# Three sums in DRAM for the experts' outputs of a token, where there were four

## The chip, the cores and the metric

The kernel runs on one NeuronCore of a Trainium2 chip, as one launch. The time is that of the device in microseconds (us): the kernel before took 3354.55 us, the median of 9 runs (3341.1 to 3369.14). One further execution was recorded by the profiler and took 3357.96 us; the durations below are from it.

## What is computed

Two transformer-like layers over `x` of 4 sequences x 2048 tokens x 256 features, float32:

```python
x = x + delta_rule_attention(layernorm(x))     # 16 heads of 16, a recurrence over the tokens
x = x + moe(layernorm(x))                      # this is the part that the change touches
x = x + state_space_scan(layernorm(x))         # state of 16, a recurrence over the tokens
x = x + quantized_linear(layernorm(x))         # values rounded to a 6-bit grid in blocks of 32

def moe(x):                                    # 32 experts, 8 of them for each token
    topk_idx, topk_w = gate(x)
    outs = down(silu(gate_proj(x)) * up(x))    # per expert; 256 -> 128 -> 256
    final = (gathered(outs, topk_idx) * topk_w).sum(1)
    return final + shared_mlp(x)
```

Each token's result in `moe` is therefore a sum of eight weighted expert outputs, of the shared network's output and of the residual `x`.

## The kernel before

The tokens are worked on in 16 blocks of 512 (128 tokens of each of the four sequences). The blocks fall into four groups of 3, 5, 5 and 3 blocks.

**First phase** (the span's first 2255 us or so). `delta_layer` does the attention of block after block. `Router.route` follows one block behind: it chooses the experts, writes the block's residual plus shared output into the first sum (`rt["sums"](i, 0)`, line 791) and copies a block of zeros into each of the other sums (lines 792 to 795). Then it scatters each token's row, eight times, into `rows`, a DRAM table that is sorted by expert (line 799, GpSimd, called POOL below). Further DMAs per group give every sum 128 spare rows of zeros and pad the table (lines 815 to 822). When a group of blocks is complete, the expert tiles of that group may begin. 160 tiles (64 of group 0 and 96 of group 1, `BEGUN`) are woven into the first phase.

**Experts.** A tile is two half tiles of 128 rows, each of one expert. `load` fetches 384 KB of weights, 128 KB of rows and each row's weight and token number per half (lines 925, 929, 930), `widen` computes the hidden layer (line 946 on TensorE, PE below; 951 on ScalarE, ACT; 952 on VectorE, DVE), and `narrow` the output (line 959 on PE). ACT scales it by the router's weight into the tile `ye` (line 964), and POOL starts an indirect DMA that *adds* the 128 rows of 256 floats to rows of a sum in DRAM (line 967):

```python
y = work.tile([P, 2, DM], F32, name="ye", bufs=self.ahead)
...
nc.gpsimd.indirect_dma_start(
    rt["sum"][g][(2 * t + n) % NACC][:, :],
    bass.IndirectOffsetOnAxis(ap=wrow[:, n, 1:2].bitcast(U32), axis=0),
    y[:, n, :], None, bounds_check=GROUPS[g] * TOK + P - 1, compute_op=ALU.add,
)
```

Such an indirect DMA is called a scatter below. Each group has `NACC` sums, and its scatters go to them in turn. Two scatters into one sum may touch the same token, so the framework lets a scatter wait until the one before it *into the same sum* has landed. That wait stands in POOL's queue, which is worked off in order. `ye` has `ahead` buffers: 2 tiles in the first phase, 6 tiles (12 scatters) in the second. ACT may write a buffer again when its scatter has landed.

**Second phase.** `last_layers` takes block after block through three stages, which are woven together. `stage_sum` (lines 1077 to 1085) loads sum 0 of a block as `x` (line 998) and then one `part` after the other, and adds them on DVE:

```python
for m in range(1, NACC):
    part = work.tile([P, NB, DM], F32, name="part", bufs=3)
    nc.sync.dma_start(part, rt["sums"](i, m))
    nc.vector.tensor_tensor(x, x, part, op=ALU.add)
    yield
```

`stage_scan` and `stage_ffn` do the last two lines of the reference; they give POOL three operations per block (lines 1094, 1095, 1147). The other 160 expert tiles (groups 2 and 3) are woven into blocks 0 to 12. Blocks 13 to 15 are group 3's own: `stage_sum` of block 13 reads sums to which the very last tile adds.

Within both phases the order of the instructions on each engine is set by a scheduler, which works from a timeline of its own. Plain DMAs are started by SyncE (SP); all engines' queues are in order.

Of the kernel before, what the change touches and what calls it, by code (L numbers as in the profile page):

```python
# [49 lines left out]
BEGUN = [64, 96, 0, 0]  # L50
NROW = NE * REG + P
DR = DM + 2 * NE
NACC = 4
XB = 2
AHEAD = 0.8
KC = 4
# [565 lines left out]
class Router:  # L622
# [8 lines left out]
    def __init__(self, ctx, sh, layer, rt):  # L631
# [125 lines left out]
        def stage_route(i, x, count, views):  # L757
# [33 lines left out]
            nc.sync.dma_start(rt["sums"](i, 0), x)  # L791
            for m in range(1, NACC):
                layer.beside(nc.sync.dma_start(
# [14 lines left out]
        def route(i, x):  # L808
            g = GROUP_OF[i]
            if i == GFIRST[g]:  # L810
# [7 lines left out]

                for m in range(NACC):
                    layer.beside(nc.sync.dma_start(  # L820
# [58 lines left out]
class Experts:  # L879
# [9 lines left out]
    def group(self, g, lag, lo, hi):  # L889
# [65 lines left out]
        def narrow(t):  # L955
# [7 lines left out]
            for n in range(2):  # L963
# [3 lines left out]
# [3 lines that stand above are left out]
# [13 lines left out]
def last_layers(ctx, sh, layer, xout, rt):  # L983
# [93 lines left out]
    def stage_sum(i):  # L1077
        x = load_x(i)
        x_of[i] = x
# [3 lines that stand above are left out]
# [93 lines left out]
def block_kernel(ctx: ExitStack, tc: tile.TileContext, a: dict, out: bass.AP):  # L1176
# [6 lines left out]
        "sum": [  # L1183
            [keep.tile([n * TOK + P, DM], F32, name=f"sum{g}_{m}") for m in range(NACC)]
            for g, n in enumerate(GROUPS)
# [156 lines left out]
```

## Time and profile before

| | us |
|---|---|
| median of 9 runs | 3354.55 (3341.1 to 3369.14) |
| the profiled execution | 3357.96 |
| its span, from the first to the last instruction | 3356.2 |
| busy in the span: PE / DVE / ACT / POOL | 2792.8 / 2010.2 / 1812.6 / 1735.2 |
| scatters (line 967), all on POOL | 640, 1043.4 us busy |
| last scatter started / landed | 3166.9 / 3174.2 |

"Idle before, releaser" in the profile is the idle time of an engine ahead of a group of instructions, and what ended most of it. "SPq" and "POOLq" are the queues of SP and POOL. The chain that ended last is followed back from the last instruction, at each step to what released it. A scatter's own row shows only POOL's work for it; when its data has landed is seen from the semaphore that each scatter raises 16 times, the last of which tells that it is done.

### The profile page before, as it was taken

The numbers are of one execution on the slowest core, as the hardware profiler recorded it, in microseconds if no ns is written. First come the engines' busy times: TensorE is split into PE (matmuls) and PEld (weight loads), VectorE is DVE, ScalarE is ACT, GpSimd is POOL, SyncE is SP. The second block draws the span as 40 slices with busy tenths as digits, with TensorE's granted clock in tenths as the row PEclk, the third lists the DMA queues.
The fourth block names the chain that finished last, engine by engine and source line by source line (L and its number), as shares of the span: only waits on it lengthen the run. The fifth ranks groups of instructions, "written<-read, shape, count | busy, mean of one in ns | idle before, by whom it ended". The sixth has DMA issues, their size and how long they took to land. (4 is left out here: it accounts for less than half of the span.)

```text
span 3356.2 us, 72319 instructions
## 1 busy us (share of the span) xinstructions
PE 2792.8 (83%) x24564; PEld 2095.6 (62%) x24564; DVE 2010.2 (60%) x4958; ACT 1812.6 (54%) x3640; POOL 1735.2 (52%) x1235
## 2 busy tenths in 40 slices
PE   5768886899999878999999888875898998899644
PEld 2446564676777656777677566763676777667522
DVE  4787675665656656576565645434667442764466
ACT  3544453555656555566565544543665764577432
POOL 0003224456475552746647455566667887568611
PEclk7778787999999998999999889987999999999876
DMA  2334446888898887988888889788999999999800
GB/s 86 61 64 113 109 112 182 201 217 216 202 261 219 220 217 196 233 215 226 222 196 250 203 243 233 192 251 264 305 297 293 278 302 307 302 251 295 218 24 19
DMA packets 788810, 695.92 MB, mean 207 GB/s; under 512 B 482312, under 2 KB 672024, under 8 KB 785304
## 3 DMA queue, kind: packets, MB, share of 16 engines
q1 hardware_dynamic: 669432, 522.25, 54.6%
q0 software_dynamic: 116736, 167.85, 24.0%
q8 instruction: 195, 3.19, 0.4%
q14 instruction: 175, 1.43, 0.1%
q10 hardware_dynamic: 2272, 1.19, 0.1%
HBM read 472.41 MB, written 267.53 MB: 220 GB/s over the span
## 5 line engine op out<-in xcount | busy, mean ns | idle before, releaser
L967 POOL DMA_INDIRECT sum<-ye,wrow x640 | 1043.4, 1630 | 707.9 <-ACT ye L964 498.6
L799 POOL DMA_INDIRECT rows<-xn,rows x512 | 544.3, 1063 | 420.8 <-issue 180.2
L946 PE MATMUL gu<-xe,we 128*128 128x128 f32 x5120 | 672.6, 285 | 43.2 <-ACT xe L936 35.9
L946 PEld LDWEIGHTS gu<-xe,we 128*128 128x128 f32 x5120 | 629.3, 198 | 98.6 <-ACT xe L936 47.0
L959 PE MATMUL py<-we,he 128*128 128x256 f32 x1280 | 360.5, 406 | 78.6 <-DVE he L952 78.1
L964 ACT ACTIVATE ye<-py,wrow 128x256 f32<-128x256 f32 x640 | 268.3, 472 | 242.0 <-PE py L959 165.9
L952 DVE TENSOR_TENSOR he<-he,gu 128x256 f32<-128x256 f32 x320 | 133.0, 416 | 422.1 <-ACT he L951 421.4
L934 PE MATMUL px<-ident,xg 128*128 128x128 f32 x1280 | 227.7, 289 | 120.5 <-DMA xg<-rows 116.1
L959 PEld LDWEIGHTS py<-we,he 128*128 128x128 f32 x1280 | 229.9, 197 | 138.3 <-DVE he L952 94.1
L934 PEld LDWEIGHTS px<-ident,xg 128*128 128x128 f32 x1280 | 163.8, 147 | 200.2 <-DMA xg<-rows 83.4
L936 ACT COPY xe<-px 128x512 f32<-128x512 f32 x320 | 188.2, 588 | 176.1 <-PE px L934 174.9
L951 ACT ACTIVATE he<-gu 128x256 f32<-128x256 f32 x320 | 123.5, 386 | 259.6 <-PE gu L946 257.0
L348 DVE TENSOR_TENSOR kqd<-kq,hmask 128x512 f32<-128x512 f32 x256 | 168.0, 687 | 91.3 <-PE pg L358 84.7
L263 DVE SCALAR_TENSOR_TENSOR cy<-pre,convw,cy 128x512 f32<-128x512 f32 x288 | 214.4, 749 | 3.5
L247 PE MATMUL proj<-xt,wqkv 128*128 128x512 f32 x384 | 203.7, 658 | 3.3 <-DVE rq L310 3.0
L505 PE MATMUL c<-vkm,tm 64*64 64x64 f32 x4096 | 178.2, 235 | 11.8 <-ACT vkm L490 9.5
L549 DVE TENSOR_TENSOR state<-sps,same 128x512 f32<-128x512 f32 x254 | 164.3, 681 | 32.3 <-PE sps L542 31.8
L505 PEld LDWEIGHTS c<-vkm,tm 64*64 64x64 f32 x4096 | 152.0, 146 | 49.1 <-issue 25.3
L358 PE MATMUL pg<-kqd,kq 64*32 64x128 f32 x4096 | 139.9, 301 | 42.7 <-ACT gk L365 29.3
L542 PE MATMUL sps<-ro,kr 64*128 64x128 f32 x2032 | 165.1, 308 | 7.1 <-ACT ro L535 7.1
L542 PEld LDWEIGHTS sps<-ro,kr 64*128 64x128 f32 x2032 | 138.8, 208 | 40.5 <-issue 15.8
L143 DVE BATCH_NORM_STATS2 st<-x 128x6 f32<-128x256 f32 x256 | 92.1, 414 | 104.0 <-DMA x<-in_x 102.7
(206 smaller groups left out, 4941.3 us busy)
## 6 DMA issues: line engine op xcount, KB each, us to landing
we<-in_wexp SPq DMA_DIRECT2D x640, 384.0 KB
xg<-rows SPq DMA_DIRECT2D x640, 128.0 KB
sum<-in_blank SPq DMA_DIRECT2D x48, 512.0 KB
part<-sum SPq DMA_DIRECT2D x48, 512.0 KB
rows<-in_zeros SPq DMA_DIRECT2D x132, 160.0 KB
x<-in_x SPq DMA_DIRECT2D x32, 512.0 KB
gscr<-gk SPq DMA_DIRECT2D x64, 256.0 KB
lq<-gscr SPq DMA_DIRECT2D x64, 256.0 KB
```

What stands on the lines that cost most here:

```text
L247: nc.tensor.matmul(ps, wqkv[:, k, w, c * P : (c + 1) * P], xt[:, k, :], start=(k == 0), stop=(k == NC2 - 1),)
L263: nc.vector.scalar_tensor_tensor(y, pre[:, :, k : k + T], convw[:, w, c, k : k + 1], y, op0=ALU.mult, op1=ALU.add,)
L348: nc.vector.tensor_tensor(kqd, kq[:, u0 + du, c].rearrange("p b t w -> p b (t w)") .unsqueeze(2).broadcast_to([P, NB, HH, 2 * C]), hmask.u ...
L505: nc.tensor.matmul(c0[rows, :, p * 32 : (p + 1) * 32], tmk[rows, p].rearrange("p b t -> p (b t)"), vkm[rows, :, p].rearrange("p w r d -> p ...
L542: nc.tensor.matmul(sps[h][:, h2, c, :], kr[rows, h2, c * P : (c + 1) * P], ro[rows, c * P : (c + 1) * P], start=(i == 0 and k == 0 and h2 ...
L799: layer.beside(nc.gpsimd.indirect_dma_start(views[((i - GFIRST[GROUP_OF[i]]) * NB + b) * TOPK + k], bass.IndirectOffsetOnAxis(ap=rows[:, b ...
L934: nc.tensor.transpose(px[:, c, n, :], xg[:, n, c * P : (c + 1) * P], ident)
L936: nc.scalar.copy(xt, px)
L946: nc.tensor.matmul(gu[:, v, n, :], w[n][:, o : o + P], xt[:, c, n, :], start=(c == 0), stop=(c == NC2 - 1),)
L959: nc.tensor.matmul(py[:, n, :], h[:, n, :], w[n][:, 4 * P :], start=True, stop=True)
L964: nc.scalar.activation(y[:, n, :], py[:, n, :], AF.Copy, scale=wrow[:, n, 0:1])
L967: nc.gpsimd.indirect_dma_start(rt["sum"][g][(2 * t + n) % NACC][:, :], bass.IndirectOffsetOnAxis(ap=wrow[:, n, 1:2].bitcast(U32), axis=0), ...
```

## The change

`NACC` is 3. A group has three sums; scatters go to them in turn. Per block one copy of zeros, one load of a part and one DVE addition fall away (16 of each), and per group one small copy of zeros (4). A scatter waits for the third one before it, where it waited for the fourth.

```diff
--- before.py
+++ after.py
@@ -50,7 +50,7 @@
 BEGUN = [64, 96, 0, 0]
 NROW = NE * REG + P
 DR = DM + 2 * NE
-NACC = 4
+NACC = 3
 XB = 2
 AHEAD = 0.8
 KC = 4
```

## The prediction

> **What bounds the kernel now.** I read the page first, then busy time by stage, then the chain, then POOL's waits and timeline. By stage, the second phase is the full one:
>
> ```profile
> 2255.00:3175.00 920.00, 794.91 (x4732) 616.57 (x4731) 501.81 (x1072) 554.61 (x981) 652.63 (x398) 0.94 1.03 284
> 3175.00:3356.00 181.00, 80.86 (x204) 39.76 (x204) 122.81 (x247) 47.94 (x63) 24.39 (x10) 0.69 0.11 39
> ```
>
> (columns: stretch, length, then busy us and count of PE, weight loads, DVE, ACT, POOL; granted clock, DMA share, GB/s). PE is busy 86% of it and the DMA queues together over 100%: loads are always waiting there. After 3175 only the last three blocks are left, a chain of DVE and PE work that the scatters do not touch. So whatever delays the last scatter delays the end by as much. The chain that ended last says the same:
>
> ```profile
> 3089.61 34.93 DMA sum<-ye,wrow x6
> ...
> 3125.04 19.24 DMA sum<-ye,wrow x3
> ...
> 3159.38 3.57 DMA sum<-ye,wrow
> ...
> 3166.90 7.33 DMA sum<-ye,wrow
> 3174.24 4.71 DMA part<-sum
> ```
>
> (start, us, what.) From 3090 to 3174 the end hangs on scatters alone; before that it is mostly expert matmuls with a few waits for loads. Now POOL, which starts the scatters:
>
> ```profile
> L967 POOL DMA_INDIRECT sum<-ye,wrow x640 | 1043.4, 1630 | 707.9 <-ACT ye L964 498.6
> ```
>
> ```profile
> 3101.04 1.55 POOL L967 DMA_INDIRECT sum<-ye,wrow  x1 [0.30 <-DMA sum<-ye,wrow]
> 3102.89 1.55 POOL L967 DMA_INDIRECT sum<-ye,wrow  x1 [0.31 <-DMA sum<-ye,wrow]
> 3105.32 1.55 POOL L967 DMA_INDIRECT sum<-ye,wrow  x1 [0.88 <-DMA sum<-ye,wrow]
> ...
> 3141.80 1.55 POOL L967 DMA_INDIRECT sum<-ye,wrow  x1 [1.34 <-DMA sum<-ye,wrow]
> ```
>
> A scatter costs POOL 1.55 us and some 0.30 between two: back to back, one in 1.86 us. A wait for an earlier scatter shows as the longer gaps (0.88, 1.34). They are small, because four sums are just enough, as the next part shows.
>
> **The price of a scatter's turn.** From the semaphores I took each scatter's time from its start on POOL to its last raise. In 2255 to 3139 it is 3.64 us at the least, 6.6 on average, 5.6 to 7.4 for eight in ten; from 3141 to 3164, when the expert loads have ended, 3.6 to 3.9, with one at 4.9. The shortest distance between a scatter's landing and the start of the fourth after it is 0.73 us, and about a tenth of the scatters after 2500 stand at that value: they were held by this wait. With four sums a scatter can start every (6.6 + 0.73) / 4 = 1.83 us, which POOL's own 1.86 covers. **With three it is (6.6 + 0.73) / 3 = 2.44 us**: the wait becomes the bound wherever POOL has scatters back to back.
>
> Would fewer scatters in flight land sooner? Those that found none in flight (19, second phase) took 7.0 us at the median, those that found two (197) 6.7. So it is not their own queue. It is the load beside them: a fit over the second phase gives 4.3 us for a share of one of the SP queue's packets, and 0.1 per scatter in flight. That share is 0.70; if the experts slow by 3 to 4% and a fifth of the block loads goes (4 KB packets, 0.10 of it), I estimate 0.65, hence 0.2 us less, and some more for the pauses: 6.3 us, and (6.3 + 0.73) / 3 = **2.34 us**.
>
> A rule speaks against this price. The Trainium skill's page "DMA: Bandwidth & Descriptors", section "Anatomy of one DMA — SWDGE (gpsimd) path", has some 2.0 us plus bytes / 436,000 for a DMA started by GpSimd. For 128 KB that is an estimated 2.3 us; with POOL's 1.55 a scatter would land after 3.85, three sums would allow one in 1.53 us, and the wait would cost nothing. The row at 3159.38 (3.57) agrees with the page for a quiet chip; the 6.6 under load does not, and I go by that.
>
> **Where it is paid.** POOL's scatters by stretch (columns: stretch, length, busy us and count, clock, DMA, GB/s):
>
> ```profile
> 2325.00:2395.00 70.00, 31.42 (x20) 0.86 1.01 286
> ...
> 2605.00:2675.00 70.00, 52.00 (x34) 1.00 1.07 278
> 2675.00:2745.00 70.00, 55.66 (x36) 0.95 1.12 304
> 2745.00:2815.00 70.00, 52.53 (x35) 1.00 1.11 303
> 2815.00:2885.00 70.00, 35.23 (x22) 0.92 1.04 301
> ```
>
> At 2.34 a stretch of 70 us holds 30. Three stretches have 34 to 36; most others have 20 to 27 and room. In the timeline POOL has two long runs without an idle gap over 3 us.
>
> *Run A*, 2580 to 2840: 122 scatters, 9 other operations. Summing, for each pair of neighbours closer than 2.34 us, what is missing to it gives 43 us; taking the run's mean distance (260 / 122 = 2.13) instead, 26. After it POOL idles 7.6, 10.0, 20.7 and 15.3 us, 54 in all, so it catches up. But `ye` lets POOL lie only 12 scatters behind, 12 x 2.34 = 28 us. From 2500 to 2750 the lag is already 10 us at the median and 22 at the ninth tenth. So 6 to 18 us of the 43 fit, and for the other 25 to 37 ACT stands at line 964. Behind it in ACT's queue are the copies of `xe` and `xt` and the activations; PE waits for those and for banks. PE's own waits for `xg` loads in this phase (48 us) shrink by what the loads gain. I book 15, between nothing and 37.
>
> *Run B*, 3032 to 3168: 63 scatters, 49 of them before the loads end at 3139, after which 1.86 holds again. The missing distance sums to 18 us; 8 if the landing falls to 5.6; 22 at 2.44, and up to 40 with what run A leaves over. It ends at the last scatter, so it is paid in full. I book 20.
>
> In the first phase a scatter would be held in 15 of 309 cases, 15 us in sum and not in a row; POOL there waits for other things (180 us for its row scatters' issue alone). I book 1, between 0 and 15. The instruction order of both programs shows the new wait at a distance of three throughout, other POOL work staying between the same neighbours within a few places.
>
> **What falls away.** 16 copies of zeros in the first phase: each is 16 packets of 32 KB, 1.5 us per DMA engine, so 24 us of 2255, 1.1%, and 16 x 0.58 = 9 us of SP's queue. No wait in the trace is put down to them for more than 0.3 us; PE (busy 85%) and the attention's chain hide them. I book -3, between 0 and -24.
>
> 16 DVE additions of 1.22 us (20 us) and as many loads of 512 KB; DVE waited 35 us for parts, in 8 places. DVE is busy 55% in the second phase, and two of its longest part waits (9 and 8 us) are on the chain early on, where POOL does not yet bound. I book -4 there. After the last landing, blocks 13 to 15 lose three additions, 3.7 us of a stretch in which DVE is the busiest engine, and one landing overlaps more: -5. Together -9, between 0 and -30. The four small copies: nothing, no wait is put down to them.
>
> Sum: +15 + 20 + 1 - 3 - 9 = **+24 us**. Against the profiled execution, 3357.96 + 24 = 3382; the median of the runs stands 3.4 below that execution, so **3379 us**.
>
> **Rivals.**
>
> *The landing comes down (faster).* If scatters land within 3 x 1.86 - 0.73 = 4.85 us, three sums hold POOL's pace and the wait costs nothing; that is the deciding point. For it: 3.6 when quiet, 3.64 at the least under load. Against it: 5.6 at the first tenth, and no less when alone in flight. Then only the gains are left, -12 to -20: about 3339.
>
> *The full price.* The landing stays at 6.6, the distance is 2.44: 54 us in run A, of which 44 do not fit, less 10 that shorter load waits return; 32 in run B, carry included; gains 12. +54: 3409. For it: variation, since a late scatter holds the two sums behind it in POOL's order as well.
>
> *The idle time absorbs run A and half of run B.* PE's 48 us of load waits and POOL's 54 us after run A take up A; B costs 12; gains 12: 3355, no change that can be told (a measurement of this kernel tells about 0.3%, 10 us, from nothing).
>
> That the change does not do what it says is excluded: the instruction order shows 32 part loads, 32 copies and the shorter wait.
>
> **Chances.** Forecast (3365 to 3395) 0.50; full price 0.20; absorbed 0.16; faster 0.14. Faster by over 0.3% 0.14, within 0.16, slower 0.70. The range runs from the faster rival to a little above the full price, 3340 to 3415; beyond lie half of the faster case, and the part of the full price in which run A is not absorbed at all (37 + 40 - 4).
>
> **What would show it.** Right: POOL's back-to-back distance at 2.2 to 2.5 us in the stretches with expert loads, the idle ahead of line 967 put down to scatters up from 52 to over 150 us, ACT's wait at line 964 for scatters up, the last scatter at 3190 to 3215, and the stretch from its landing to the end at 175 to 180 us. Wrong: a landing time below 5.5 us in the second phase; a last scatter before 3170; a first phase that moves by over 15 us, which would be the scheduler's doing, of which I price nothing.

## The result, and the profile after

The changed kernel took 3375.0 us, the median of 20 runs (3357.91 to 3385.76). Beside it the kernel before was run again, and over all its 62 runs its median is 3348.53. The ratio is 1.0077 (95% interval 1.0061 to 1.0092): **26 us slower**, where 24 were forecast, inside the range. The profiled execution of the changed kernel took 3369.51, 5.5 below its median, and that of before 9.4 above its median, so that the two traces are only 11.5 us apart. A size that is read from one trace is therefore rough.

By stage, columns as in the prediction (stretch, length, busy of PE, weight loads, DVE, ACT, POOL, clock, DMA share, GB/s), the changed kernel:

```profile
2255.00:3175.00 920.00, 787.32 (x4677) 605.42 (x4677) 481.20 (x1061) 556.91 (x986) 645.33 (x393) 0.94 1.02 273
3175.00:3367.00 192.00, 88.11 (x228) 46.16 (x228) 120.87 (x247) 47.95 (x63) 32.70 (x15) 0.68 0.13 41
```

The second phase begins at 2256 in both traces. In the same 920 us PE does less, and the DMA queues move 273 GB/s instead of 284. Of these 11 GB/s some 7 are the 13 part loads that are gone from this stretch; the rest goes with expert work that ends later. The scatters by stretch of 70 us show what holds it:

```profile
2325.00:2395.00 70.00, 31.33 (x19) 0.92 1.03 307
2605.00:2675.00 70.00, 47.38 (x30) 1.00 1.08 286
2675.00:2745.00 70.00, 44.78 (x29) 0.98 1.05 269
2745.00:2815.00 70.00, 46.18 (x29) 1.00 1.07 282
2815.00:2885.00 70.00, 39.87 (x25) 0.80 0.96 257
```

Where there were 34 to 36 there are 30, 29 and 29, the number that a distance of 2.34 us allows; the emptier ones shown have 19 instead of 20 and 25 instead of 22. POOL's timeline in one of them (start, length, then in brackets the idle time before and what ended it):

```profile
2703.76 1.55 POOL L967 DMA_INDIRECT sum<-ye,wrow  x1 [0.30 <-DMA sum<-ye,wrow]
2706.25 1.55 POOL L967 DMA_INDIRECT sum<-ye,wrow  x1 [0.94 <-issue]
2709.80 1.55 POOL L967 DMA_INDIRECT sum<-ye,wrow  x1 [2.00 <-DMA sum<-ye,wrow]
2712.20 1.55 POOL L967 DMA_INDIRECT sum<-ye,wrow  x1 [0.85 <-DMA sum<-ye,wrow]
2714.75 1.55 POOL L967 DMA_INDIRECT sum<-ye,wrow  x1 [1.00 <-ACT ye L964]
```

The gaps of 0.85 to 2.0 us in a row were single events before. The chain that ended last, followed back, now runs through scatters for 14% of the span (4% before). By line, first of the kernel before, then of the changed one:

```profile
PE gu L946 5%; DMA xg<-rows 4%; DMA sum<-ye,wrow 4%; PE py L959 3%; PE psf L1162 1%; PE px L934 1%; DVE qy L1026 1%; PE psy L1140 1%; PE pz L1100 1%; DMA we<-in_wexp 1%; DVE xn L152 1%; SPq L841 1%; DMA rows<-xn,rows 1%; SPq L838 1%; DMA part<-sum 1%
```

```profile
DMA sum<-ye,wrow 14%; PE gu L946 1%; PE py L959 1%; PE psf L1162 1%; DMA we<-in_wexp 1%; DVE xn L152 1%; DMA xg<-rows 0%; PE pz L1100 0%; PE psy L1140 0%; DVE qd L1040 0%; DVE qy L1026 0%; DVE qr L1037 0%; PE pd L1112 0%; DVE qr L1036 0%; DVE qsc L1022 0%
```

Near its end, in order of time:

```profile
3089.86 14.47 DMA sum<-ye,wrow x4
3104.49 36.24 DMA sum<-ye,wrow x8
3140.76 12.08 DMA sum<-ye,wrow x3
...
3182.51 5.34 DMA sum<-ye,wrow
3187.86 3.76 DMA part<-sum
```

The last scatter lands at 3187.9 instead of 3174.2; from there to the end it is 179.9 us instead of 182.0.

POOL's waits for an earlier scatter, over the whole span, doubled. First before, then the changed kernel (engine and line, what it waited for: us in total, times, the longest):

```profile
POOL sum L967 <- DMA sum<-ye,wrow: 51.7, 135, 1.7
```

```profile
POOL sum L967 <- DMA sum<-ye,wrow: 104.4, 145, 3.8
```

### The profile page after: what moved, and what is told of

It reads as the page before. It is cut to its first block, busy times and chain, and to the rows that moved or that the text cites. A ratio compares the mean times of both kernels' runs of the same rounds, so it can differ in the third digit from the quotient of the medians.

```text
span 3367.7 us, 72285 instructions
## 1 busy us (share of the span) xinstructions
PE 2792.2 (83%) x24564; PEld 2096.0 (62%) x24564; DVE 1985.7 (59%) x4942; ACT 1814.2 (54%) x3648; POOL 1737.9 (52%) x1235
## 5 line engine op out<-in xcount | busy, mean ns | idle before, releaser
L934 PE MATMUL px<-ident,xg 128*128 128x128 f32 x1280 | 220.6, 288 | 110.8 <-DMA xg<-rows 89.6
```

Source lines behind the costliest of these rows:

```text
L934: nc.tensor.transpose(px[:, c, n, :], xg[:, n, c * P : (c + 1) * P], ident)
```

## The experiments

The first eight ran on two other chips, e1 to e4 on one and e5 to e8 on another, on which the kernel before takes 3606 and 3614 us, where it takes 3349 on the first. The span's granted clock in these eight traces is 0.87 to 0.88 (0.86 in e7_two), against 0.90, and the first phase lasts some 2500 us instead of 2255. In the kernel of e5, which has four sums in the second phase, that phase's scatters take the same 821 us there as in the kernel before on the first chip. So ratios are compared, each with the kernel before on the same chip; what the second phase alone costs may carry over in us rather than in per cent, which changes little below (59 us for 55). The last four ran together on one chip, where the kernel before takes 3364.5.

Two counts come from the semaphores: a scatter is *held* where it starts less than 0.85 us after the landing it waits for, and the *scatter stretch* is the time from group 2's first scatter to the last of all. In the traces of e1 to e8 semaphore raises are missing: in the second phase 11 to 14 of a scatter's 16 are recorded on average, in the other six traces nearly all. A landing may therefore look too early there, and a held scatter be missed; the counts of e1 to e8 are rough.

**e1_turn3: the wait alone.**

```diff
-                    rt["sum"][g][(2 * t + n) % NACC][:, :],
+                    rt["sum"][g][(2 * t + n) % 3][:, :],
```

> Four sums are still zeroed and read, but scatters go to three of them in turn, so that only the wait is changed. My theory (the wait for the third scatter before is the whole price, the work saved gives 9 to 12 us back): +35 us against before, +30 to +45, ratio about 1.010, and a second phase whose back-to-back scatters stand 2.2 to 2.3 us apart. Rival A (the time comes from the scheduler's other order, which any change of this size would bring): within 10 us of before. Rival B (the work saved is worth nothing, so the wait alone costs what the change costs): +26.

Measured: 1.0163 (1.0134 to 1.0193), on that chip +59 us, well over the 30 to 45 expected. The edit also changes the order in which the scheduler puts the instructions, which no run separates from the wait. Two other runs speak against it as the cause: e5 and f2 below, whose order differs from that of before as well (64 and 29 of POOL's 1241 operations stand at another place, 73 in e1), moved by -0.03% and +0.08%.

**e2_work3: the saved work alone.**

```diff
-NACC = 4
+NACC = 3
...
-            [keep.tile([n * TOK + P, DM], F32, name=f"sum{g}_{m}") for m in range(NACC)]
+            [keep.tile([n * TOK + P, DM], F32, name=f"sum{g}_{m}") for m in range(4)]
...
-                    rt["sum"][g][(2 * t + n) % NACC][:, :],
+                    rt["sum"][g][(2 * t + n) % 4][:, :],
```

> Three sums are zeroed and read, but scatters go to four; the fourth sum is never zeroed and never read, so a quarter of the expert outputs is left out of the result. Only the saved copies, loads and additions are left of the change. My theory: -9 us against before, -4 to -20, most of it after the last scatter and at the start of the second phase. Rival (they are hidden behind other work throughout): within 3 us of before.

Measured: 0.9931 (0.9910 to 0.9952), -25 us, more than the 4 to 20 expected. The two parts of the change add up to +0.94%, the change itself is +0.77%, inside what the intervals leave open. Each is well over what was booked: the wait +36 us (1.1%), the work -12 (0.4%).

**e3_turn3_g2, e4_turn3_g3, e5_turn3_g01: the wait in one group of scatters at a time.**

```diff
-                    rt["sum"][g][(2 * t + n) % NACC][:, :],
+                    rt["sum"][g][(2 * t + n) % (3 if g == 2 else 4)][:, :],
```

(e4 has `g == 3`, e5 `g < 2`.)

> Four sums throughout, but the scatters of group 2 alone (192 of 640, the first long run of the second phase) go to three of them. By the prediction +15 us (0 to 37). By the profile of the changed kernel, in which the outputs of blocks 1 to 5 leave up to 44 us later and that of block 7 at the same time as before, the idle time after the run absorbs it: 0 to +6.

> Four sums throughout, but the scatters of group 3 alone (128 of 640, the last run, after which the end follows) go to three of them. My theory: +20 us (13 to 35), paid in full since nothing comes after the run that could absorb it; with e3 it adds up to e1. Rival (the whole second phase runs at POOL's pace, each scatter costs alike): 128/320 of e1, +14, and e3 +21.

> Four sums, but the scatters of groups 0 and 1 (320 of 640, all in the first phase or at its end) go to three of them. My theory: +1 us, -5 to +8, since scatters there come in pairs with pauses between them. Rival (the first phase lost what the saved copies gave it, 18 us at 1972 in the profile of the changed kernel, to the new wait): +10 to +18.

Measured: group 2 1.0105 (1.0078 to 1.0131), +38 us; group 3 1.0058 (1.0032 to 1.0084), +21; groups 0 and 1 0.9997 (0.9971 to 1.0022). Together 1.60%, which is e1's 1.63. Group 3 costs what was booked, the first phase nothing, and group 2, to which run A belongs, over twice the 15, and well over the 0 to 6 that this run's own theory had. (A group has more scatters than the prediction's run in it: 192 against 122, and 128 against 63.)

The traces say why the first phase is free: there 17 of 314 scatters were held in the changed kernel. In the second phase it was 159 of 314, before 52 of 312.

**e6_six and e7_two: more and fewer sums.**

```diff
-NACC = 4
+NACC = 6
```

(e7 has 2.)

> Six sums. A scatter waits for the sixth before it: (6.6 + 0.73) / 6 = 1.22 us, well under POOL's 1.86, so the wait is gone; in the kernel before 52 of some 320 scatters of the second phase were held by it, for a fraction of a us. Against that 32 more copies, loads and additions. My theory: +12 us (0 to 25), the gain from the wait no more than 6 us. Rival (the four sums still cost much through the late scatters): faster than before by 5 us or more.

> Two sums. A scatter waits for the second before it: (5.8 to 6.0 + 0.73) / 2 = 3.3 us for each of the 320 scatters of the second phase, 1060 us where the phase has 920. My theory: +140 to +200 us in the second phase, less 20 for the work saved: +120 to +190, about 3490. In the first phase some cost too, since pairs of the two sums follow each other: up to 30. Rival (the landing comes down as the load does, to 4.5): +0 to +60.

Measured: six sums 1.0154 (1.0126 to 1.0182), +56 us; two sums 1.0825 (1.0789 to 1.0862), +298. With six no scatter is held. Of the waits on POOL, e1 against e6, columns as above:

```profile
POOL sum L967 <- DMA sum<-ye,wrow: 95.4, 127, 2.6
```

```profile
POOL sum L967 <- DMA sum<-ye,wrow: 1.2, 4, 0.3
```

And still it is slower, by more than the 0 to 25 us expected. So the wait that four sums leave costs nothing that can be told from this, and the price of a sum more is the work: 32 more copies, loads and additions cost 56 us, 16 fewer gave 25 back. That is some 1.6 to 1.75 us for each set. With two sums POOL waits twice in the time of a pair of scatters:

```profile
2936.48 1.56 POOL L967 DMA_INDIRECT sum<-ye,wrow  x1 [2.31 <-DMA sum<-ye,wrow]
2938.35 1.56 POOL L967 DMA_INDIRECT sum<-ye,wrow  x1 [0.30 <-issue]
2942.86 1.56 POOL L967 DMA_INDIRECT sum<-ye,wrow  x1 [2.95 <-DMA sum<-ye,wrow]
```

6.4 us for two, 3.2 each, as (5.6 + 0.73) / 2 has it with that trace's mean landing time. The price of a scatter was forecast rightly: e7's scatter stretch of 1054 us is 3.3 us for each of its 320. But +120 to +190 had set these 1060 us against the 920 of the whole phase. The scatters before take 821 of them, so the stretch alone is 233 us longer.

**e8_three_ye12: more buffers behind the wait.**

```diff
-            y = work.tile([P, 2, DM], F32, name="ye", bufs=self.ahead)
+            y = work.tile([P, 2, DM], F32, name="ye", bufs=2 * self.ahead)
```

(with `NACC = 3`)

> The changed kernel with twice the ye buffers, 12 tiles in the second phase (4 in the first). In the changed kernel ACT stood idle 134 us for ye buffers, where before it was 35. By the prediction's step the buffers keep POOL from lying more than 12 scatters behind, and what does not fit stops ACT and PE: with 24, run A is absorbed, so the time falls by up to 15 us against the changed kernel, to about +11 against before. Rival (run A is absorbed anyway and the end waits for the last scatter, which more buffers do not bring forward): +22 to +28 against before, as the changed kernel.

Measured: 1.0076 (1.0049 to 1.0103), nothing gained. ACT's wait for scatters had grown with the change, and did vanish here; first the kernel before, then the changed one, then e8, all of the span:

```profile
ACT ye L964 <- DMA sum<-ye,wrow: 35.3, 18, 8.4
```

```profile
ACT ye L964 <- DMA sum<-ye,wrow: 131.0, 50, 5.9
```

```profile
ACT ye L964 <- DMA sum<-ye,wrow: 3.9, 8, 0.5
```

But another stop was already there. `wrow` holds the token numbers that the scatter reads, so its buffers (12 tiles) also come free only when a scatter has landed, and SP, which loads them at line 930, stands with all expert loads behind it: again the changed kernel, then e8, and the kernel before:

```profile
SPq L930 <- DMA sum<-ye,wrow: 69.5, 67, 5.7
```

```profile
SPq L930 <- DMA sum<-ye,wrow: 61.8, 55, 4.3
```

```profile
SPq L930 <- DMA sum<-ye,wrow: 21.2, 11, 5.1
```

The rival of that run holds in its number. Its reason, that run A would be absorbed anyway, does not: e3 had shown the opposite. That `wrow` is why nothing was gained is argued from these rows; no run has more buffers of both.

**f1_three_due7 and f2_four_due7: group 2 finished earlier.** In the changed kernel SP stood 16 us at the load of block 8, the first that needs group 2's sums (its line 998 waited 45.9 us for scatters in two places, before 28.4 in one). Was group 2's price paid there?

```diff
         late, n = [0] * nblk, 0
+        DUE = [GFIRST[0], GFIRST[1], GFIRST[2] - 1, GFIRST[3]]
...
-                -(-(sum(left[: g + 1]) - n) // (GFIRST[g] - i))
-                for g in range(NGRP) if GFIRST[g] > i
+                -(-(sum(left[: g + 1]) - n) // (DUE[g] - i))
+                for g in range(NGRP) if DUE[g] > i
```

(f1 also has `NACC = 3`)

> The changed kernel with one edit: the tiles of group 2 are due one block earlier (14 per block in blocks 0 to 4, 13 in 5 and 6, then 10 or 11), so that its last scatter lands well before block 8, the first that reads group 2's sums. In the changed kernel SP stood 16 us at that load, with all expert loads queued behind it, which it did not before. My new theory (the price of group 2 is paid at this border, not through full ye buffers): about +0.4% against before, where the changed kernel has +0.8%. Rival (the price is paid by throughput all along): +0.7 to +0.9%, as without the edit.

> Control for the run above: the kernel before, four sums, with the same edit. There SP does not stand at the border, so the new theory has within 0.2% of before. Rival (the earlier due time helps by itself, for instance since it fills an emptier first half of the phase): faster by 0.3% or more; then the run above has to be read against this one.

Measured: f1 1.0078 (1.0050 to 1.0106), f2 1.0008 (0.9987 to 1.0029). The experiment decides nothing: the scheduler made of f1 the order of the changed kernel (the same on POOL, ACT and SP throughout), and in f2 group 2 ended no earlier in its phase either. f1 is a second measurement of the change, +0.78%. Whether a part of group 2's price is paid at the border stays open; e8, whose SP stood 13 us there, gives no separate number.

**f3_3344 and f4_2244: fewer sums where the wait is free.**

```diff
-NACC = 4
+NACC = (3, 3, 4, 4)
...
-            for m in range(1, NACC):
+            for m in range(1, NACC[GROUP_OF[i]]):
...
-                    rt["sum"][g][(2 * t + n) % NACC][:, :],
+                    rt["sum"][g][(2 * t + n) % NACC[g]][:, :],
```

(and so in the other places that count sums; f4 has `(2, 2, 4, 4)`)

> Three sums for groups 0 and 1, whose scatters had room for the shorter wait (-0.03% in its run), four for groups 2 and 3. Half of the saved copies, loads and additions of the change are had (8 of 16): half of the -0.69% of that run, -0.35%, -0.2 to -0.5. Rival (only what is saved near the end of the kernel counts, blocks 8 to 15): within 0.1%.

> Two sums for groups 0 and 1, four for groups 2 and 3: 16 copies, loads and additions saved, as many as by the change. With two sums throughout 15 of 314 scatters of groups 0 and 1 were held, so the wait should cost next to nothing there: -0.6%, -0.3 to -0.8, the fastest of all. Rival (with two tiles of ye buffers the held scatters stop the first phase): 0 to +0.5%.

Measured: f3 **0.9928 (0.9902 to 0.9955)**, faster than both kernels; f4 0.9949 (0.9925 to 0.9974). f3 has half of e2's savings and as much of a gain, more than the 0.2 to 0.5% expected: 3 us a set (1.9 to 4.1 by its interval), so that 1.6 to 1.75 is no fixed price. Whether the savings of blocks 0 to 7 count for more is open. f4 is not the fastest, as it was expected to be: 71 of its 316 scatters of groups 0 and 1 were held, and its second phase begins at 2280 us, where that of f3 begins at 2251 and that of f2, with four sums, at 2242. That takes back what the other eight copies, loads and additions gave: its scatter stretch is 785 us, f3's 800 and f2's 822.

The traces side by side. Each is a single execution, so a difference of 10 us in one says little. Landing and share are taken from the start of the second phase to the end of the expert loads:

| | sums for the scatters of groups 2, 3 | part loads | scatter stretch, us | held, groups 2 and 3 | mean landing, us | share of SP's queue |
|---|---|---|---|---|---|---|
| before | 4, 4 | 48 | 821 | 52 | 6.60 | 0.715 |
| e5 | 4, 4 | 48 | 821 | 31 | 6.36 | 0.702 |
| e2 | 4, 4 | 32 | 784 | 26 | 6.46 | 0.698 |
| f3 | 4, 4 | 40 | 800 | 37 | 6.57 | 0.717 |
| f2 | 4, 4 | 48 | 822 | 45 | 6.54 | 0.717 |
| f4 | 4, 4 | 32 | 785 | 45 | 6.58 | 0.711 |
| e1 | 3, 3 | 48 | 858 | 131 | 6.05 | 0.692 |
| changed | 3, 3 | 32 | 840 | 159 | 6.12 | 0.706 |
| e6 | 6, 6 | 80 | 882 | 0 | 6.49 | 0.689 |
| e7 | 2, 2 | 16 | 1054 | 195 | 5.58 | 0.564 |

With the scatters on four sums, the stretch goes down with the part loads (f3 by 20 us, e2 and f4 by 36), and it is longer in e6. The first phase, from which the copies of zeros fall away, is in none of them shorter by more than 5 us than with 48 copies on the same chip: the second phase begins at 2506 us in e2 (32 copies) and at 2477 to 2486 in e1, e3 and e4 (48, the same chip), and on e5's chip (2514 there) the earliest to begin is e6 (80 copies), at 2463.

## Why the prediction was right, and where only in sum

*The sign and the mechanism held.* The run with the wait alone is 1.6% slower, the run with the saved work alone is faster, and the wait costs only in the second phase, where POOL has scatters back to back.

*The distance* was put at 2.34 us from a landing of 6.3. The landing was 6.1; the median distance was 2.20 us in group 2 and 2.14 in group 3, the mean of those under 4 us 2.26. The count by stretch (30, 29, 29) came out at the forecast 30.

*Run B* (booked 20): the whole of group 3 cost 21 in e4 (12 to 30 by the interval). *The first phase* (booked 1) cost nothing in e5.

*Run A was mis-sized:* 15 booked "between nothing and 37", +38 measured in e3 (28 to 47) for the whole of group 2. The step that failed is the last one: from the 25 to 37 us for which ACT would stand down to 15, on the strength of PE's shorter waits for loads and of POOL's 54 us of idle time after the run. e3's trace can be laid beside the four that have four sums in group 2 (before, f2, e4, e5), each counted from group 2's first scatter. Group 2's last scatter starts 41 to 46 us later in e3. Some 15 us of that arise in the first 60 scatters, ahead of run A, where the prediction saw room and booked nothing (how much of it is the scheduler's order is open). By the 49th scatter of group 3, 27 to 34 us are left, and at the last of all 30 to 32 (against before, f2 and e5). So the pauses gave back 9 to 16 us, and no more: POOL idles 56 us between these two scatters in e3, and 65 to 73 in the other four. Most of its longer pauses there are ahead of line 1147, for DVE's work on the blocks, and they moved with the run; first before, then e3, from group 2's last scatter on:

```profile
POOL x L1147 <- DVE xn L152: 36.2, 3, 20.7
```

```profile
POOL x L1147 <- DVE xn L152: 34.1, 2, 22.5
```

More room in `ye` changed nothing (e8). Whether it would have if `wrow` had been deeper too was not tried.

*The saved work was mis-sized the other way:* -12 booked, -25 measured. I had called the part loads nearly hidden since few waits are put down to them. In a phase whose queues are full at 285 GB/s 512 KB take 1.84 us of everybody's loads, without a wait of their own in the profile. That is near the 1.6 to 1.75 us per set of e2 and e6, and under f3's 3. By the traces above the gain lies in the scatter stretch, and none of it shows in the first phase, so nothing here shows the copies of zeros as its source. How much of it is the load and how much the DVE addition was not taken apart; that it is the load is argued.

So the sum, +24 for +26, owes something to two errors that cancelled: +36 should have been about +55 on this chip (1.63% of 3349), and -12 about -23 (0.69%). That the total came out within 2 us is luck.

*Of the signs that I named,* the distance (in group 2; group 3's median is just under the 2.2 to 2.5), ACT's wait at line 964 (35 to 131 us), the unmoved start of the second phase and the last stretch (179.9 us, forecast 175 to 180) came true. Two did not: POOL's idle time put down to scatters is 104 us, not over 150, and the last scatter starts at 3182.5, not after 3190. For the first, part of the same stop may be booked under another name: between 2255 and 3190 us POOL's waits for ACT's `ye` rose from 29.0 to 44.6 us. The second fits the profiled execution, which is 5.5 us faster than the median, and the larger gain from the loads. Neither was tested.

*The rivals.* The landing did not come down to the 4.85 us at which three sums would be free, not even with two sums (5.6). "The full price" was nearer on the wait (66 us for run A's 44 that do not fit, less 10, and run B's 32, against 55 measured) and wrong about the distance and the gains. That idle time absorbs run A is refuted by e3.

The wait itself cannot be left out. The Trainium skill's page "DMA: Bandwidth & Descriptors", section "Rules for kernel authors", says that an accumulating DMA reads its destination and writes it later, and that another write in between is lost, so that one waits for the earlier DMA's semaphore. No run here shows such a loss, since none leaves the wait out.

## What to carry to other kernels

A ring of targets is deep enough when (landing + hand-over) / depth is below the issuing engine's own pace; take the landing from the stage that is loaded, not from a quiet one, and set the depth for each stage by itself: here 3 sums in the first phase and 4 in the second beat either number throughout. Do not count idle time that follows a saturated run in the same dependent program as slack: here it gave back 9 to 16 of some 44 us. In a stage whose DMA queues are full, a first price for a load that is removed is its bytes over the stage's rate, even where no wait carries its name (here 1.84 us; 1.6 to 3 measured for a load with its copy and addition).

## What the runs showed of the hardware

The landing time of an accumulating scatter goes with how many may be in flight more than the one trace of before told. There, scatters that found none in flight landed no sooner than others, and the fit gave 0.1 us each. Between kernels, in the traces whose semaphore raises are nearly complete, it is 6.5 to 6.6 us with four sums (before, f2, f3, f4) but 6.12 and 6.15 with three (the changed kernel, f1). SP's queue has 0.71 to 0.72 of the packets' time throughout; the prediction's 4.3 us for a share of one would make 0.05 us of that, not 0.5. The cause was not isolated. The traces with raises missing fit in: 6.5 with six sums, and 5.6 with two, at a share of 0.56. Quiet, it is 3.6 to 3.9.

On the chip with the lower clock (0.87 against 0.90 in the first phase of e5 and of before) the first phase took 2514 us against 2256, while the scatter stretch of the second phase, at the same clock of 0.96, took 821 in both. The first phase is 11% longer at a clock 4% lower, so the clock as recorded does not account for all of it; no run shows what does.
